# The transposed mask of neighbours: from 64 f16 transposes per graph to ScalarE's sign of a matrix that is already transposed

## The chip, the core and the metric

The kernel runs on one core of one Trainium2 chip. The metric is the device time of one execution in microseconds; the kernel before took 3909.36 us as the median of three runs (3884.14 to 3925.28). TensorE is called PE below, VectorE DVE, ScalarE ACT, GpSimd POOL and SyncE SP.

## The reference

For each of 16 graphs of N = 1024 nodes with 64 features there is a matrix `adj` (1024 x 1024, f32) that is zero where two nodes are not neighbours and otherwise between 0.05 and 1; its diagonal is always positive. Four layers follow one another, each on `h = relu(layernorm(x))`. The first, second and fourth are products with `adj`. The third needs the set of neighbours itself:

```python
nb = (adj_ > 0) & (~eye)[None]
m = nb.sum(-1)
rank = jnp.cumsum(nb, axis=-1) - 1
skip = jnp.where(m > T_THRESH, (m + K_DIL - 1) // K_DIL, 1)
do_dil = (skip > 1) & mask
removed = nb & do_dil[..., None] & ((rank + 1) % skip[..., None] == 0)
rem = removed | jnp.swapaxes(removed, 1, 2)
return jnp.where(rem, 0.0, adj_)
```

Of what is left, each node takes three quantiles over the features of its neighbours, weighted and summed, and a small dense network follows. The change touches the running count (`rank`) alone.

## The kernel before, in words

`direct_path` treats the graphs in six streams of work (`adjacency`, `layers`, `tail`, `gathers`, `neighbour_lists`, `sorts`). They are generators. A loop at the end of the function keeps a model of the engines' clocks (`clk`), takes the first stream that is due by DVE's modelled time and lets it issue its instructions up to its next `yield`. So the order on every engine is fixed when the kernel is built, and several graphs are in work at once: while one graph's mask is made, DVE sorts the gathered neighbours of an earlier one.

`adjacency(b)` works by blocks of 128 rows, i = 0 to 7:

- DVE makes the mask `nb` of the block in f16 (L942) and clears its diagonal (L944). PE transposes the block of `adj` in f32 (L949), ACT copies it out of PSUM into `adjt` (L950), so that `adjt[p, j, i*128 + m]` is `adj[i*128 + m, j*128 + p]`. ACT also sums the mask by halves of a row (L956), into `mn`. DVE adds these sums (L964) and works out `sf`, the numbers that tell which neighbour is dropped (L965 to L971).
- Then the running count, block by block. `flipped(i)` makes the transposed mask `nbt` of block i: eight f16 transposes of `nb` on PE into one PSUM bank (L979) and one ACT copy to SBUF (L980). `flipped(i + 1)` is issued ahead of the work on block i; `nbt` has two buffers. Eight matmuls of `nbt` by a constant staircase (`stair`, L991) give the running count in each half of the row. ACT takes the absolute distance from the count that is dropped (L995) into `gone`, DVE turns it into -1 or 0 (L1000, L1005).
- Then the keys: PE adds the mask, `gone`, its transpose and the node numbers (L1015 to L1023), ACT makes keys of the sum (L1024) and counts them (L1027), and the nodes are sorted by number of neighbours (L1034 to L1073).

`layers(b)` runs beside the last two steps. It normalises (`preln`, L848 to L858), multiplies by `adjt` twice (`messages`, L877, copied by L878), and ACT sums the rows of `adjt` in place (L1212: same shape and same memory in and out, with a sum per row). The next graph's `adjacency` starts once these, and this graph's keys, have been issued. PSUM has three rings: `t` (tiles `pt`, one bank, three buffers), `t2` (two banks, two buffers) and `tm`.

At the end a flag is made from `bad`, which tells of a node with too many or too few neighbours for the lists. If it is set, `general_path` computes everything again in another way.

Of the kernel before, what the change touches and what calls it, by code (L numbers as in the profile page):

```python
# [7 lines left out]
F32 = mybir.dt.float32  # L8
F16 = mybir.dt.float16
BF = mybir.dt.bfloat16  # L10
I32 = mybir.dt.int32
U16 = mybir.dt.uint16
U8 = mybir.dt.uint8
AF = mybir.ActivationFunctionType
ALU = mybir.AluOpType
AX = mybir.AxisListType

P = 128
C = 64
NB = 8  # L20
# [28 lines left out]
BIG = 1e30  # L49

E_ID, E_ONE, E_CAP, E_LOW, E_CN, E_HALF, E_Q, E_END = 0, 128, 256, 264, 272, 280, 288, 352
J_ID, J_BIG, J_OFF, J_ST, J_ROW, J_ONE, J_PI, J_NI, J_END = 0, 128, 256, 384, 896, 1920, 2048, 2176, 2184

# [7 lines left out]
def _wanted(cap, low):  # L63

    places = set()
    for m in range(low, cap + 1):
        above = (cap + 1) // 2 - (m + 1) // 2
        places |= {above + k * (m - 1) // 4 for k in (1, 2, 3)} | {above - k * (1 - m) // 4 for k in (1, 2, 3)}
    return sorted(places)
# [662 lines left out]
def direct_path(ctx: ExitStack, tc: tile.TileContext, t: dict, out: bass.AP, flag):  # L732
# [3 lines left out]
    nc = tc.nc  # L736
    x_in, adj, nodemask = t["x"], t["adj"], t["nodemask"]
    B = x_in.shape[0]

    const = ctx.enter_context(tc.tile_pool(name="const", bufs=1))  # L740
    loads = ctx.enter_context(tc.tile_pool(name="loads", bufs=2))
    graph = ctx.enter_context(tc.tile_pool(name="graph", bufs=1))
    nodes = ctx.enter_context(tc.tile_pool(name="nodes", bufs=2))
# [6 lines left out]
    tt, ts, act = nc.vector.tensor_tensor, nc.vector.tensor_scalar, nc.scalar.activation  # L750
# [4 lines left out]
    ch = const.tile([P, J_END], F16, name="eh")  # L755
    nc.scalar.dma_start(ch, t["eh"])
    identf, onesf = cf[:, E_ID:E_ID + P], cf[:, E_ONE:E_ONE + P]
    cap8, low8, cn8, half8 = (cf[:, e:e + NB] for e in (E_CAP, E_LOW, E_CN, E_HALF))
    identh, big_i, offdiag = (ch[:, e:e + P] for e in (J_ID, J_BIG, J_OFF))
    stair, pidx = ch[:, J_ST:J_ST + N // 2], ch[:, J_PI:J_PI + P]  # L760
    nid = ch[:, J_NI:J_NI + NB]
    jrow, onerow = ch[0:1, J_ROW:J_ROW + N], ch[0:1, J_ONE:J_ONE + P]
    eps = const.tile([P, 1], F32, name="eps")
    nc.vector.memset(eps, 1e-5)
    bad = const.tile([P, NB], F32, name="bad")
    nc.vector.memset(bad, 0.0)

    def weight(name, n):
        w = const.tile([n, t[name].shape[1]], F32, name=name)
        nc.gpsimd.dma_start(w, t[name])  # L770
        return w
# [46 lines left out]
    def after(dve=0.0, pe=0.0, act=0.0, lat=0.3):  # L818

        clk.dve += dve  # L820
        at = clk.dve
        if pe:
            clk.pe = at = max(clk.pe, at) + pe
        if act:
            clk.act = at = max(clk.act, at) + act
        return at + lat


    def bank(dt=F32):
        return psum.tile([P, 2048 // mybir.dt.size(dt)], dt, tag="t", name="pt", bufs=3)  # L830

    def bank2():
        return psum.tile([P, N], F32, tag="t2", name="pt2", bufs=2)
# [101 lines left out]
    def adjacency(b):  # L935
        g = state[b]
        adjt = graph.tile([P, NB, N], F32, name="adjt")
        nb = graph.tile([P, NB, N], F16, name="nb")
        mn = nodes.tile([P, 3, NB], F32, name="mn")
        for i in range(NB):  # L940
# [4 lines left out]
            for q in range(2):  # L945
                p = bank()
                for u in range(4):
                    j = 4 * q + u
# [22 lines left out]
        nc.vector.scalar_tensor_tensor(sf[:, 3], mn[:, 0], 2.0, sf[:, 2], op0=ALU.mult, op1=ALU.add)  # L971
        clk.dve += 0.9
        gone = graph.tile([P, NB, N], F16, name="gone")

        def flipped(i):
            nbt = lists.tile([P, NB, P], F16, name="nbt")
            p = bank(F16)
            for j in range(NB):
                nc.tensor.transpose(p[:, j * P:(j + 1) * P], nb[:, i, j * P:(j + 1) * P], identh)  # L979
            nc.scalar.copy(nbt, p.rearrange("p (j m) -> p j m", m=P))  # L980
            return nbt

        nbt = flipped(0)
        waiting = None
        for i in range(NB):
            following = flipped(i + 1) if i + 1 < NB else None

            p = bank2()
            for j in range(NB):
                o, e = j * P, (j // 4 + 1) * 512  # L990
                nc.tensor.matmul(p[:, o:e], nbt[:, j, :], stair[:, :e - o], start=j % 4 == 0, stop=j % 4 == 3)  # L991

            for q in range(2):
                s = slice(q * 512, (q + 1) * 512)
                act(gone[:, i, s], p[:, s], AF.Abs, bias=sf[:, 2 + q, i:i + 1], scale=2.0)  # L995
            nbt = following
            ready = after(0, pe=3.7, act=2.4, lat=3.0)
            if waiting:
                yield waiting[1]
                ts(gone[:, waiting[0], :], gone[:, waiting[0], :], sf[:, 1, waiting[0]:waiting[0] + 1], -1.0,  # L1000
                   op0=ALU.is_equal, op1=ALU.mult)
                clk.dve += 0.5
            waiting = (i, ready)
        yield waiting[1]
        ts(gone[:, waiting[0], :], gone[:, waiting[0], :], sf[:, 1, waiting[0]:waiting[0] + 1], -1.0,  # L1005
           op0=ALU.is_equal, op1=ALU.mult)
        clk.dve += 0.5
        keys_d = dram.tile([N, N], F16, name="keys_d")
        ms = nodes.tile([P, NB], F32, name="ms")
        for i in range(NB):  # L1010

            p = bank2()
            for q in range(2):
# [4 lines left out]
                for j in range(4 * q, 4 * q + 4):  # L1018
                    d = slice(j * P, (j + 1) * P)
                    nc.tensor.matmul(p[:, d], gone[:, j, i * P:(i + 1) * P], big_i, start=False,  # L1020
                                     stop=j == 4 * q + 3 and i // 4 != q)
# [5 lines left out]
            act(p, p, AF.Sign, accum_out=ms[:, i:i + 1])  # L1027
            yield after(0, pe=4.5, act=2.3) - 4.0

        mv = nodes.tile([P, NB], F32, name="mv")  # L1030
        act(mv, ms, AF.Copy, bias=512.0, scale=0.5)
        yield clk.act + 2.0
        key = nodes.tile([P, NB], F32, name="key")
        nc.vector.scalar_tensor_tensor(key, ms, 512.0, cn8, op0=ALU.mult, op1=ALU.add)  # L1034
        neg = nodes.tile([P, NB], F32, name="neg")
        ts(neg, key, -1.0, None, op0=ALU.mult)
        p = bank2()
        for q in range(2):
# [2 lines left out]
               key[:, 4 * q:4 * q + 4, None].to_broadcast([P, 4, P]), ALU.mult)  # L1041
            nc.tensor.matmul(p[:, q * 512:(q + 1) * 512], onesf, spread.rearrange("p j m -> p (j m)"),
                             start=True, stop=True)
        over = nodes.tile([P, NB], F32, name="over")
        for i in range(NB):
            sink = lists.tile([P, N], F16, tag="ab", name="sink")
            act(sink, p, AF.Sign, bias=neg[:, i:i + 1], accum_out=over[:, i:i + 1])  # L1047
# [1 line left out]
        pos = nodes.tile([P, NB], I32, name="pos", bufs=5)  # L1049
        ts(pos, over, 0.5, 511.5, op0=ALU.mult, op1=ALU.add)  # L1050

        pi = nodes.tile([P, 2, NB], I32, name="pi")
        ts(pi[:, 0], pos, P - 1, None, op0=ALU.bitwise_and)
        ts(pi[:, 1], pos, 7, None, op0=ALU.arith_shift_right)
        ph = nodes.tile([P, 2, NB], F16, name="ph")
        nc.vector.tensor_copy(ph, pi)
        low = lists.tile([P, NB, P], F16, tag="ab", name="low")
        tt(low, pidx[:, None, :].to_broadcast([P, NB, P]), ph[:, 0, :, None].to_broadcast([P, NB, P]), ALU.is_equal)
        high = nodes.tile([P, NB, NB], F16, name="high")
        tt(high, pidx[:, None, :NB].to_broadcast([P, NB, NB]), ph[:, 1, :, None].to_broadcast([P, NB, NB]),  # L1060
           ALU.is_equal)
        both = nodes.tile([P, 2, NB, NB], F16, name="both")
        tt(both[:, 0], high, nid[:, :, None].to_broadcast([P, NB, NB]), ALU.mult)
        tt(both[:, 1], high, mv[:, :, None].to_broadcast([P, NB, NB]), ALU.mult)
        p = bank()
        for i in range(NB):
            nc.tensor.matmul(p[:, :2 * NB].rearrange("p (s k) -> p s k", k=NB), low[:, i, :], both[:, :, i, :],
                             start=i == 0, stop=i == NB - 1)
        m = nodes.tile([P, NB], F32, name="m", bufs=3)
# [332 lines left out]
        done.add(("tail", b))  # L1402


    wcol = const.tile([P, 3], F32, name="wcol")
    for k, w in enumerate((0.25, 0.5, 0.25)):
        nc.vector.memset(wcol[:, k:k + 1], w)
    none = const.tile([P, 2], F32, name="none")
    nc.vector.memset(none[:, :1], BIG)
    nc.vector.memset(none[:, 1:], 0.0)  # L1410
    sizes = [max(p0 + ns * nn for l, p0, _, ns, nn in PACKS if l == k) for k in range(NPACK)]
# [9 lines left out]
    def over_graphs(step, *needs):  # L1421
# [5 lines left out]

    streams = [
        over_graphs(adjacency, ("adjt", 1), ("keys", 1), ("sorts", 3)),
        over_graphs(layers, ("rows", 0), ("tail", 3)),  # L1430
        over_graphs(tail, ("sorts", 0)),
# [23 lines left out]
                assert soonest is not None  # L1455
                clk.dve = soonest

    one = nodes.tile([P, 1], F32, name="one")
    nc.vector.tensor_reduce(one, bad, AX.X, ALU.max)
    p = bank()  # L1460
    nc.tensor.matmul(p[:1, :1], one, onesf[:, :1], start=True, stop=True)
    nc.vector.tensor_copy(flag, p[:1, :1])


@with_exitstack
# [10 lines left out]
def _constants():  # L1476

    import numpy as np

    p = np.arange(P)  # L1480
    ef = np.zeros((P, E_END), np.float32)
    ef[p, E_ID + p] = 1
    ef[:, E_ONE:E_ONE + P] = 1
    e = E_Q
    for b0, n, cap, low, *_ in GROUPS:
        ef[:, E_CAP + b0:E_CAP + b0 + n] = PLACES[b0:b0 + n]
        ef[:, E_LOW + b0:E_LOW + b0 + n] = low
        ef[:, E_HALF + b0:E_HALF + b0 + n] = (cap + 1) // 2
        for q in _wanted(cap, low):
            ef[:, e] = q  # L1490
            e += 1
    for _, _, s0, ns, nn in PACKS:
        ef[:nn, E_CAP] = s0 + ns
    ef[:, E_CN:E_CN + NB] = 512 * N + N - 1 - (p[:, None] + P * np.arange(NB))
    eh = np.zeros((P, J_END), np.float32)
    eh[p, J_ID + p] = 1
    eh[p, J_BIG + p] = 2048
    eh[:, J_OFF:J_OFF + P] = 1
    eh[p, J_OFF + p] = 0
    eh[:, J_ST:J_ST + N // 2] = p[:, None] < np.arange(N // 2)  # L1500
    eh[p, J_ST + p] = 2050
    eh[0, J_ROW:J_ROW + N] = np.arange(N) - 2047
    eh[0, J_ONE:J_ONE + P] = 1
    eh[:, J_PI:J_PI + P] = p
    eh[:, J_NI:J_NI + NB] = p[:, None] + P * np.arange(NB)
    return {**_general_constants(), "ef": ef, "eh": eh.astype(np.float16)}
# [73 lines left out]
```

## Time and profile before

| | |
|---|---|
| median of three runs | 3909.36 us |
| profiled execution | 3897.33 us, span 3895.5 us |
| mean granted PE clock | 0.689 |
| busy: DVE, POOL, PE, ACT | 3035.7, 2644.1, 2044.1, 1410.1 us |
| L979, transposes of the mask | 1024 on PE, 99.8 us busy; first at 32.2 us, last at 3341.2 us |
| L980, copies of the transposed mask | 128 on ACT, 128.2 us busy |

The profile is of one execution. A group's line gives the engine, the operation, what it writes and reads by the program's names, the shape, the count, the busy time, the mean of one in ns, and after a second bar the idle time of the engine just before these instructions and what ended it. An engine's idle time costs something only where work that sets the end waits for it. The profile releases a wait by semaphore events; "remote" and "another core or an unknown queue" mean that it found no releaser, "issue" that the engine waited for nothing that it shows. Some matmul records are missing.

### The profile page before, as it was taken

The page shows a single profiled execution, that of the slowest core. Times are in us where ns is not written, and L with a number is a line of the kernel's source. Part 1 is how long each engine was busy: PE and PEld are TensorE (multiplying, and loading weights), DVE is VectorE, ACT ScalarE, POOL GpSimd, SP SyncE. Part 2 cuts the span into 40 slices and gives each one's busy share as a digit, 9 for nine tenths or more (in the row PEclk, how much of TensorE's full clock was granted, in tenths as well). Part 3 has the DMA queues.
Part 4 walks back from the last instruction along what each step waited for, and adds up shares of the span by engine and source line. Part 5 has one row for each costly group of instructions (what it writes and reads, how often), then busy time and mean ns, then how long its engine had stood idle before and what let it go on. Part 6 is the DMA issues. An engine that isn't in the chain of part 4 may idle for free.

```text
span 3895.5 us, 32579 instructions
## 1 busy us (share of the span) xinstructions
PE 2044.1 (52%) x8483; PEld 988.9 (25%) x8483; DVE 3035.7 (78%) x7309; ACT 1410.1 (36%) x2658; POOL 2644.1 (68%) x2792
## 2 busy tenths in 40 slices
PE   6464554646654574646446474565556555741113
PEld 3222222223222232222222232232222323220101
DVE  1557878879687897888787798899699876979482
ACT  5444334243433434333332443443344433430000
POOL 1077576776667686776776777777778686777781
PEclk8666667677676686676666777767677676765555
DMA  2313234152423425242341524243343423232121
GB/s 89 124 39 115 50 99 117 45 172 46 141 68 101 120 65 154 70 125 69 106 106 45 175 51 153 56 142 80 100 119 104 116 55 123 68 105 58 42 52 55
DMA packets 237348, 362.43 MB, mean 93 GB/s; under 512 B 126848, under 2 KB 128496, under 8 KB 237152
## 3 DMA queue, kind: packets, MB, share of 16 engines
q1 hardware_dynamic: 156912, 255.00, 19.0%
q0 software_dynamic: 80096, 104.70, 13.5%
q8 instruction: 69, 1.13, 0.1%
q14 instruction: 127, 1.04, 0.1%
q10 hardware_dynamic: 144, 0.56, 0.0%
HBM read 245.26 MB, written 114.81 MB: 92 GB/s over the span
## 4 chain that ended last, share of the span: by engine, by line
DVE 42%; issue 14%; PE 12%; another core or an unknown queue 9%; ACT 8%; POOL 8%; DMA 5%; SPq 0%; DVEq 0%; ACTq 0%; POOLq 0%
DVE other L1308 12%; DVE raw L1308 11%; POOL raw L1275 6%; PE pt L877 5%; DVE most L1117 4%; ACT adjt L1212 2%; DVE found L1103 2%; DVE agg L1327 2%; ACT sink L1047 2%; DMA k<-keys_d,node 1%; DMA raw<-h_d,index 1%; PE pt L901 1%; DVE k L1112 1%; DVE nb L942 1%
## 5 line engine op out<-in xcount | busy, mean ns | idle before, releaser
L1275 POOL DMA_INDIRECT raw<-h_d,index x1984 | 2148.8, 1083 | 559.0 <-issue 533.1
L1308 DVE TENSOR_TENSOR other<-raw 128x512 f32<-128x512 f32 (+11 forms) x816 | 536.7, 688 | 151.7 <-DMA raw<-h_d,index 113.9
L877 PE MATMUL pt<-adjt,ha 128*65 128x512 f32 (+1 forms) x1024 | 485.4, 635 | 44.6 <-DVE ha L1199 30.6
L919 POOL COPY gate<-mark 1x1 f32<-1x1 f32 x477 | 163.9, 344 | 416.2 <-DVE mark L917 369.3
L949 PE MATMUL pt<-ef,a 128*128 128x128 f32 x1024 | 207.5, 360 | 320.8 <-ACT adjt L950 129.6
L1308 DVE TENSOR_TENSOR raw<-other 128x512 f32<-128x512 f32 (+10 forms) x464 | 355.9, 792 | 5.8 <-DVE other L1308 0.6
L991 PE MATMUL pt<-eh,nbt 128*128 128x512 f16 (+3 forms) x1024 | 213.8, 365 | 266.5 <-ACT nbt L980 192.2
L1117 DVE MAX8 most<-k 128x8 uint16<-128x1024 uint16 x208 | 255.4, 1228 | 13.2 <-DVE k L1112 3.3
L949 PEld LDWEIGHTS pt<-ef,a 128*128 128x128 f32 x1024 | 157.7, 185 | 408.2 <-issue 180.6
L1024 ACT ACTIVATE nb<-pt 128x1024 f16<-128x1024 f32 x128 | 130.6, 1020 | 317.1 <-remote 118.4
L877 PEld LDWEIGHTS pt<-adjt,ha 128*65 128x65 f32 (+1 forms) x1024 | 148.1, 148 | 364.1 <-issue 360.1
L950 ACT COPY adjt<-pt 128x512 f32<-128x512 f32 x256 | 139.1, 583 | 250.0 <-remote 146.4
L956 ACT ACTIVATE nb<-nb 128x512 f16<-128x512 f16 x256 | 159.6, 629 | 179.3 <-DVE nb L942 70.2
L1308 DVE TENSOR_TENSOR raw<-other,raw 128x640 f32<-128x640 f32 (+3 forms) x448 | 216.5, 494 | 4.9
L1308 DVE TENSOR_TENSOR raw<-raw,other 128x128 f32<-128x128 f32 (+7 forms) x496 | 211.5, 436 | 6.1
L1020 PE MATMUL pt<-eh,gone 128*128 128x128 f16 x1024 | 129.7, 257 | 162.7 <-DVE gone L1000 76.5
L878 ACT COPY big<-pt 64x1024 f32<-64x1024 f32 (+1 forms) x32 | 32.2, 1007 | 496.1 <-PE pt L877 300.6
L1308 DVE TENSOR_TENSOR other<-other,raw 128x128 f32<-128x128 f32 (+4 forms) x448 | 201.4, 460 | 4.2
L1384 PE MATMUL tm<-at,ha 128*64 128x512 f32 x512 | 174.1, 785 | 50.0 <-DMA at<-adjt_d 44.4
L1103 DVE MAX8 found<-k 128x8 f32<-128x1024 f16 x128 | 156.3, 1221 | 51.2 <-DMA k<-keys_d,node 51.2
L991 PEld LDWEIGHTS <-nbt 128*128 128x128 f16 x1024 | 105.0, 116 | 359.4 <-ACT nbt L980 203.2
L1347 POOL DMA_INDIRECT res<-agg_d,pos x128 | 135.7, 1060 | 74.9 <-DMA agg_d<-agg 37.4
(182 smaller groups left out, 4350.6 us busy)
## 6 DMA issues: line engine op xcount, KB each, us to landing
a<-in_adj_dram SPq DMA_DIRECT2D x64, 1024.0 KB
adjt_d<-adjt SPq DMA_DIRECT2D x64, 1024.0 KB
at<-adjt_d SPq DMA_DIRECT2D x128, 512.0 KB
keys_d<-nb SPq DMA_DIRECT2D x64, 512.0 KB
raw<-h_d,index POOLq DMA_INDIRECT x1984
x<-in_x_dram SPq DMA_DIRECT2D x16, 256.0 KB
h_d<-h SPq DMA_DIRECT2D x16, 256.0 KB
agg_d<-agg SPq DMA_DIRECT2D x16, 256.0 KB
```

Of the source, the lines that this page charges most:

```text
L877: nc.tensor.matmul(p[p0:p0 + n, s], h[:, j, :n], adjt[:, j, s], start=j == 0, stop=j == NB - 1)
L919: nc.gpsimd.tensor_copy(opened[:, k % 2:k % 2 + 1], slots[:, k % 8:k % 8 + 1])
L949: nc.tensor.transpose(p[:, u * P:(u + 1) * P], a[:, j * P:(j + 1) * P], identf)
L950: nc.scalar.copy(adjt[:, 4 * q:4 * q + 4, i * P:(i + 1) * P], p.rearrange("p (u m) -> p u m", m=P))
L956: act(nb[:, i, s], nb[:, i, s], AF.Copy, accum_out=mn[:, q, i:i + 1])
L991: nc.tensor.matmul(p[:, o:e], nbt[:, j, :], stair[:, :e - o], start=j % 4 == 0, stop=j % 4 == 3)
L1103: nc.vector.max(out=found[:, o:o + 8], in_=src)
L1117: nc.vector.max(out=most, in_=less.bitcast(U16))
L1275: nc.gpsimd.indirect_dma_start(raw[:, s, i * C:(i + 1) * C], None, h_ds[b % 3], bass.IndirectOffsetOnAxis(ap=g["index"][:, at:at + 1], axi ...
L1308: tt(view(two[to], *((i, vi) if greater else (j, vj)), w), view(two[s], i, vi, w), view(two[u], j, vj, w), ALU.max if greater else ALU.min)
L1347: nc.gpsimd.indirect_dma_start(res[:, i, :], None, g["agg_d"], bass.IndirectOffsetOnAxis(ap=g["pos"][:, i:i + 1], axis=0))
L1384: nc.tensor.matmul(p[q * C:(q + 1) * C, :], ha[:, j, :], even(ats[j], q), start=j == 0, stop=j == NB - 1)
```

## The change

`flipped(i)` takes ACT's sign of block i of `adjt`. As `adjt` keeps the diagonal and the mask `nb` doesn't, block i's own diagonal would be counted: one more matmul per block, of minus the identity by the staircase, takes it out again. The sign of a negative entry would be -1, where the mask has 0; so ACT sums the signs as it goes, DVE compares the sum of all with the number of neighbours plus the diagonal, and any difference sets the flag for the general path. To make room for the new constant and sums, several small tiles get one buffer instead of two, and three small constants share a tile.

```diff
-    identh, big_i, offdiag = (ch[:, e:e + P] for e in (J_ID, J_BIG, J_OFF))
+    identh, big_i, offdiag, minus_i = (ch[:, e:e + P] for e in (J_ID, J_BIG, J_OFF, J_NEG))
...
-    eps = const.tile([P, 1], F32, name="eps")
+    cols = const.tile([P, 8], F32, name="cols")
+    eps, none, wcol = cols[:, :1], cols[:, 1:3], cols[:, 3:6]
...
+    over_all = const.tile([P, NB], F32, name="over_all")
+    nc.vector.memset(over_all, 0.0)
...
+        signs = nodes.tile([P, NB], F32, name="signs", bufs=1)
...
         def flipped(i):
             nbt = lists.tile([P, NB, P], F16, name="nbt")
-            p = bank(F16)
-            for j in range(NB):
-                nc.tensor.transpose(p[:, j * P:(j + 1) * P], nb[:, i, j * P:(j + 1) * P], identh)
-            nc.scalar.copy(nbt, p.rearrange("p (j m) -> p j m", m=P))
+            act(nbt, adjt[:, :, i * P:(i + 1) * P], AF.Sign, accum_out=signs[:, i:i + 1])
             return nbt
...
-                nc.tensor.matmul(p[:, o:e], nbt[:, j, :], stair[:, :e - o], start=j % 4 == 0, stop=j % 4 == 3)
+                nc.tensor.matmul(p[:, o:e], nbt[:, j, :], stair[:, :e - o], start=j % 4 == 0,
+                                 stop=j % 4 == 3 and j != i)
+                if j == i:
+                    nc.tensor.matmul(p[:, o:e], minus_i, stair[:, :e - o], start=False, stop=j % 4 == 3)
...
+        tt(signs, signs, mn[:, 2], ALU.subtract)
+        tt(over_all, over_all, signs, ALU.add)
...
-        mv = nodes.tile([P, NB], F32, name="mv")
+        mv = nodes.tile([P, NB], F32, name="mv", bufs=1)
...
-    one = nodes.tile([P, 1], F32, name="one")
-    nc.vector.tensor_reduce(one, bad, AX.X, ALU.max)
+    one = nodes.tile([P, 2], F32, name="one", bufs=1)
+    nc.vector.tensor_reduce(one[:, :1], over_all, AX.X, ALU.add)
+    ts(one[:, :1], one[:, :1], -1.0, float(B * NB), op0=ALU.mult, op1=ALU.add)
+    nc.vector.tensor_reduce(one[:, 1:], bad, AX.X, ALU.max)
+    tt(one[:, :1], one[:, :1], one[:, 1:], ALU.add)
     p = bank()
-    nc.tensor.matmul(p[:1, :1], one, onesf[:, :1], start=True, stop=True)
-    nc.vector.tensor_copy(flag, p[:1, :1])
+    nc.tensor.matmul(p[:1, :1], one[:, :1], onesf[:, :1], start=True, stop=True)
+    ts(flag, p[:1, :1], 1.0, None, op0=ALU.min)
```

The tiles `key`, `neg`, `over`, `pi`, `ph`, `high` and `both` get one buffer as `mv` does.

More of the change, by code (lines that the diff above doesn't have):

```diff
@@ L51 @@
 E_ID, E_ONE, E_CAP, E_LOW, E_CN, E_HALF, E_Q, E_END = 0, 128, 256, 264, 272, 280, 288, 352
-J_ID, J_BIG, J_OFF, J_ST, J_ROW, J_ONE, J_PI, J_NI, J_END = 0, 128, 256, 384, 896, 1920, 2048, 2176, 2184
+J_ID, J_BIG, J_OFF, J_ST, J_ROW, J_ONE, J_PI, J_NI, J_NEG, J_END = 0, 128, 256, 384, 896, 1920, 2048, 2176, 2184, 2312
 PLACES = [21, 19, 17, 16, 15, 13, 12, 11]
@@ L1028, in adjacency @@
             yield after(0, pe=4.5, act=2.3) - 4.0
-        mv = nodes.tile([P, NB], F32, name="mv")
+        mv = nodes.tile([P, NB], F32, name="mv", bufs=1)
         act(mv, ms, AF.Copy, bias=512.0, scale=0.5)
         yield clk.act + 2.0
-        key = nodes.tile([P, NB], F32, name="key")
+        key = nodes.tile([P, NB], F32, name="key", bufs=1)
         nc.vector.scalar_tensor_tensor(key, ms, 512.0, cn8, op0=ALU.mult, op1=ALU.add)
-        neg = nodes.tile([P, NB], F32, name="neg")
+        neg = nodes.tile([P, NB], F32, name="neg", bufs=1)
         ts(neg, key, -1.0, None, op0=ALU.mult)
@@ L1043, in adjacency @@
                              start=True, stop=True)
-        over = nodes.tile([P, NB], F32, name="over")
+        over = nodes.tile([P, NB], F32, name="over", bufs=1)
         for i in range(NB):
@@ L1050, in adjacency @@
         ts(pos, over, 0.5, 511.5, op0=ALU.mult, op1=ALU.add)
-        pi = nodes.tile([P, 2, NB], I32, name="pi")
+        pi = nodes.tile([P, 2, NB], I32, name="pi", bufs=1)
         ts(pi[:, 0], pos, P - 1, None, op0=ALU.bitwise_and)
         ts(pi[:, 1], pos, 7, None, op0=ALU.arith_shift_right)
-        ph = nodes.tile([P, 2, NB], F16, name="ph")
+        ph = nodes.tile([P, 2, NB], F16, name="ph", bufs=1)
         nc.vector.tensor_copy(ph, pi)
@@ L1058, in adjacency @@
         tt(low, pidx[:, None, :].to_broadcast([P, NB, P]), ph[:, 0, :, None].to_broadcast([P, NB, P]), ALU.is_equal)
-        high = nodes.tile([P, NB, NB], F16, name="high")
+        high = nodes.tile([P, NB, NB], F16, name="high", bufs=1)
         tt(high, pidx[:, None, :NB].to_broadcast([P, NB, NB]), ph[:, 1, :, None].to_broadcast([P, NB, NB]),
            ALU.is_equal)
-        both = nodes.tile([P, 2, NB, NB], F16, name="both")
+        both = nodes.tile([P, 2, NB, NB], F16, name="both", bufs=1)
         tt(both[:, 0], high, nid[:, :, None].to_broadcast([P, NB, NB]), ALU.mult)
@@ L1402, in tail @@
         done.add(("tail", b))
-    wcol = const.tile([P, 3], F32, name="wcol")
     for k, w in enumerate((0.25, 0.5, 0.25)):
         nc.vector.memset(wcol[:, k:k + 1], w)
-    none = const.tile([P, 2], F32, name="none")
     nc.vector.memset(none[:, :1], BIG)
@@ L1497, in _constants @@
     eh[p, J_BIG + p] = 2048
+    eh[p, J_NEG + p] = -1
     eh[:, J_OFF:J_OFF + P] = 1
```

## The prediction

> **What bounds the kernel now.** I read the page first, for busy shares and the chain, then the list of waits of VectorE (DVE), then the groups by form around the change, then a table of windows that cut each graph's stage of the change out of the span, and last the timeline of the first such stage.
>
> ```profile
> PE 2044.1 (52%) x8483; PEld 988.9 (25%) x8483; DVE 3035.7 (78%) x7309; ACT 1410.1 (36%) x2658; POOL 2644.1 (68%) x2792
> ...
> DVE 42%; issue 14%; PE 12%; another core or an unknown queue 9%; ACT 8%; POOL 8%; DMA 5%; SPq 0%; DVEq 0%; ACTq 0%; POOLq 0%
> ```
>
> DVE leads in busy time and on the chain. One execution of 16 graphs takes 3895.5 us, so a graph passes about every 220 us (the stages below start that far apart), 190 of them DVE work. Every engine works off a fixed order, so what counts is where DVE waits:
>
> ```profile
> DVE other L1308 <- DMA raw<-h_d,index: 113.9, 17, 25.7
> DVE stat L853 <- ACT mid L851: 96.3, 14, 16.8
> DVE stat L856 <- ACT stat L854: 64.3, 9, 19.0
> DVE gone L1000 <- ACT gone L995: 52.5, 10, 15.7
> ```
>
> (us in total, times, longest.) Only the last of these belongs to the stage of the change. With 6.4 us "issue" before L1000 and 1.7 us before L1005 it is 60.6 us, the most that a faster stage could give DVE directly. In the timeline these waits lie in four graphs: 30.6 us in the first, about 24 in the second, 4.2 in the eleventh, 1.6 in the fourteenth; in twelve of sixteen graphs DVE never waits for `gone`. The two long ones (15.69 and 13.44 us) are not the transposes' either: ScalarE (ACT) is held just ahead by `big` L878, which waits for the messages' matmuls L877. Windows cut around the stage of the third to the sixteenth graph (786 us together) have DVE busy 719 us, 91%. Two of them:
>
> ```profile
> 2445.00:2501.00 56.00, 25.77 (x164) 15.03 (x164) 50.71 (x136) 27.61 (x50) 39.01 (x40) 0.67 0.27 56
> 2655.00:2704.00 49.00, 22.19 (x147) 12.63 (x146) 47.89 (x132) 20.32 (x34) 39.41 (x39) 0.71 0.25 42
> ```
>
> (window, length, busy us and instructions of PE, PEld, DVE, ACT, POOL, granted clock, DMA share, GB/s.) PE and ACT have about half of the stage free. After it the wait goes the other way: PE's L1020 waits for DVE's L1000 and L1005, 115.4 us in 24 times. So a `gone` that ACT finishes earlier is not used earlier. The rows that the change deals in:
>
> ```profile
> L991 PE MATMUL pt<-eh,nbt 128*128 128x512 f16 x256 | 122.8, 480 | 258.8 <-ACT nbt L980 192.2 <-issue 35.5 <-ACT mid L851 16.7
> L979 PE MATMUL pt<-eh,nb 128*128 128x128 f16 x1024 | 99.8, 254 | 54.0 <-ACT adjt L950 30.8 <-issue 18.7 <-ACT x L1378 4.5
> L980 ACT COPY nbt<-pt 128x1024 f16<-128x1024 f16 x128 | 128.2, 1013 | 79.5 <-remote 54.8 <-PE pt L979 14.8 <-PE pt L991 4.7
> L1212 ACT ACTIVATE adjt<-adjt 128x1024 f32<-128x1024 f32 x128 | 133.2, 1044 | 0.0
> L1212 ACT ACTIVATION_READ_ACCUMULATOR adjt<-adjt 128x1 f32 x128 | 24.2, 189 | 0.0
> ```
>
> **What the skill says.** "ScalarE: Activation LUTs", What ACT_TABLE_LOAD costs: an activation passes one element per cycle whatever the function, 186 ns + 0.833 ns per element with immediate operands, so about 1039 ns for 1024. The trace agrees: 1044 ns (L1212), 1019 ns for the Sign of L1027. Same page, Table sets: cheap functions such as relu, copy and abs sit in every set. Sign is not named there, but the trace has loads only at the square root (17, L854), the tanh (16, L1192) and the start, though Sign runs at L1027 and L1047 in every graph; the built order of the changed kernel has no load more. "TensorE: Matmul & The Clock Gate", HAM clock gate: the clock halves after some 3.4 us of idleness and recovers after as much work. The trace agrees in kind: eight transposes span 0.61 us at 48.94 and 1.06 us at 44.02, eight L991 matmuls 1.25 us at 47.85 and 2.31 us at 41.92.
>
> **The change, part by part.** Apart from what follows, the built orders of all five engines are the same instruction by instruction; POOL's and SP's are identical.
>
> 1. PE loses 1024 f16 transposes (L979) and their weight loads: 99.8 and 81.6 us busy, per step of eight 0.6 us warm to 1.0 cold. It gains 128 matmuls of minus identity by staircase, one per step, of 512, 384, 256 or 128 columns. The four widths of L991 cost 122.8 + 103.1 + 83.4 + 64.5 = 373.8 us for 1024, so 128 cost 46.7, 0.15 us (1.25/8) to 0.3 us (2.31/8) per step. Net -53 us of PE. PE is not the bound; I count 0. Bounds: 0 to the whole 31.5 us that the first rival works out.
>
> 2. ACT: 128 copies out of PSUM become 128 Signs of `adjt` with a sum. No row shows a Sign of strided f32 from SBUF. From below: no dearer than the copy. From above: L1212's rows added, 1044 + 189 = 1233 ns, 0.22 more than 1013. In sequence they overlap: two copies take 1.91 us at 40.87, so the second starts 0.90 after the first; eight L1212 with their sums take 8.32 us in the chain, 1.04 each. I take +0.14 us each, 1.1 per graph, 18 in all (bounds 0 and 28). The stride I cost at nothing: L950 writes the same strided pattern in 583 ns, L887 and L1391 a plain one in 580 and 584. The 18 us lie beside DVE work in 12 of 16 graphs; where DVE waits for `gone`, they are 1 us per graph. Queued behind a Sign on ACT are the two Abs (L995) and sometimes L851 or L854 of the layers, for which DVE waits in this stage only in the first two graphs (4.1, 2.9 and 2.3 us).
>
> 3. The waits: ACT stood idle before L980 for 79.5 us, nearly all of it for PE; Sign waits for ACT's own earlier writes only. The buffer of two rows ago is free because the Abs ahead in the queue has waited for the matmuls that read it. But the two Abs right behind need the staircase of the same PE, so the wait moves one instruction on. What is left: where PE is late, the first staircase starts without two transposes and a copy ahead of it (about 1.5 to 2 us earlier), given back at 0.14 per step. Where ACT is late (PE waits 192.2 us for `nbt`, 48 times) it is 0.14 later. I count -1 us over the first two graphs for this and +1 for step 2.
>
> 4. DVE gains two operations on 128x8 per graph (`signs` and `over_all`). The 128x8 ops at 40.22 to 41.50 take 0.16 to 0.17 us and start up to 0.21 apart when each needs the last: 0.4 per graph, 6.4 in all. They stand behind the last L1005, whose wait covers the last Sign, so they add no wait. DVE is the bound: all 6.4 counted. At the end three small operations more: 0.6.
>
> 5. PSUM ring `pt`: eight allocations fewer per graph. No wait for `pt` on an L980 release shows, so 0. Single buffers for `mv`, `key`, `neg`, `over`, `pi`, `ph`, `high`, `both`: the old reader is a graph (220 us) back, 0. The constants' DMA grows by 128 of 2184 columns and lands before its first use: 0. Scheduler clock: the entries that order the streams are untouched.
>
> Sum: 0 - 1 + 1 + 6.4 + 0.6 = +7 us, against this execution's 3897.33 us (span 3895.5 and 1.8 around it) 3904; the median of the runs, 3909.36, lies 12 above that execution, and I carry the difference over: 3916, no change that can be told.
>
> **Rivals.** (a) Faster: the stage's chain does hold DVE. All waits for `gone` but those behind the messages go: 60.6 - 15.7 - 13.4 = 31.5, giving 3909 + 7 - 31.5 = 3885. For: ACT stood 79.5 us before L980. Against: twelve graphs without a wait. To pass 1% a share of the 160 us of L853 and L856 waits would have to shrink too; a quarter gives 3845. (b) Slower: PE goes cold. With fewer instructions between waits for `nbt` the staircases run at the half clock: 2.31 + 0.3 = 2.6 us per step, where ACT's step, a Sign and two Abs (1.04 + 1.27), is 2.3. From there PE decides; against the 2.2 of before (0.90 + 1.27) a step is 0.45 longer, 3.6 us per graph, 58 if none of it is covered: 3909 + 7 + 58 = 3974. For: the clock is only 0.62 to 0.79 in these windows. Against: cold steps exist now and cost 2.31 + 1.0, more than 2.6. (c) ACT's upper bound, all on the path: 3909 + 7 + 28 = 3944, still within 1%. (d) The sum of signs doesn't match and the general path runs as well: far slower, no row prices it. Against: the sum is over whole numbers and the diagonal is positive in these inputs.
>
> **How the numbers follow.** Forecast 0.52, (a) 0.18, (b) 0.16, (c) 0.12, (d) 0.02. A measurement tells about 1% from no change (the three runs before span 3884 to 3925). Of the forecast 0.48 falls within 1% and 0.02 on each side; of (a) 0.11 is faster by more; of (c) 0.03 slower by more; (b) and (d) are slower. So 0.13, 0.64, 0.23. The range 3862 to 3970 holds the forecast, (c), the nearer part of (a) and the milder half of (b), and leaves out about 2 in 10.
>
> **What would show it.** Right: Sign near 1.04 us plus 0.19 and no more table loads; PE busy some 50 us less; PE's waits for `nbt` about as long; the wait before Sign gone and longer before L995; DVE busy about 6 us more, its waits for `gone` still in the first graphs. Wrong: a Sign of 1.5 us or more, a granted clock lower by 0.03 and staircases mostly near 2.3 us, or DVE's waits for L851, L854 and `gone` changed by over 40 us together.

## The result and the profile after

Over 20 runs each the changed kernel takes 3891.72 us and the kernel before 3898.16 us (medians): ratio 0.9987, with a 95% interval of 0.9965 to 1.0009, that is -14 to +3.5 us, no difference that can be told. (The median of the three runs known before the prediction, 3909.36, lay high among the twenty.) On two further, steadier chips one series each gives 1.0007 (0.9999 to 1.0015) and 1.0009 (1.0003 to 1.0016) of about 3660 us, or +3 us; the second of them is clear of its own noise, by 1 to 6 us. That the change is near nothing holds. The numbers put on it, +7 us and a time of 3916 us, do not: +7 lies outside all three intervals.

The page of the changed kernel, busy time and chain:

```profile
PE 2010.3 (52%) x7587; PEld 934.0 (24%) x7587; DVE 3040.5 (78%) x7345; ACT 1424.2 (37%) x2786; POOL 2650.6 (68%) x2792
...
DVE 42%; issue 16%; POOL 10%; PE 10%; another core or an unknown queue 9%; ACT 9%; DMA 4%; SPq 0%; DVEq 0%; ACTq 0%; POOLq 0%
```

PE is busy 33.8 us less (2044.1 before), the weight loads 54.9 less, ACT 14.1 more, DVE 4.8 more, and DVE keeps its 42% of the chain. DVE's waits, the rows that answer to those of before:

```profile
DVE stat L858 <- ACT mid L856: 105.6, 11, 36.3
DVE other L1316 <- DMA raw<-h_d,index: 103.6, 13, 25.8
...
DVE gone L1006 <- ACT gone L1001: 35.9, 8, 17.0
...
DVE stat L861 <- ACT stat L859: 30.4, 6, 14.1
```

L1006 is the old L1000, L858 the old L853, L861 the old L856. The wait for `gone` fell from 52.5 to 35.9 us and that for L861 from 64.3 to 30.4, while L858 rose by 9.3: one profile of each, and such rows move by tens of us between profiles of one kernel (L858: 105.6 us here, 67.2 in a later profile of the changed kernel on another chip). The groups of the change, by form:

```profile
L983 ACT ACTIVATE nbt<-adjt 128x1024 f16<-128x1024 f32 x128 | 134.9, 1055 | 0.1
L994 PE MATMUL pt<-eh,nbt 128*128 128x512 f16 x256 | 129.0, 504 | 322.1 <-ACT nbt L983 256.1 <-issue 63.4 <-PE pt L994 2.5
L1001 ACT ACTIVATE gone<-pt,sf 128x512 f16<-128x512 f32 x256 | 161.6, 685 | 104.7 <-remote 35.1 <-PE pt L994 27.0 <-DVE other L1316 11.6
...
L983 ACT ACTIVATION_READ_ACCUMULATOR nbt<-adjt 128x1 f32 x128 | 25.4, 198 | 0.0
L997 PE MATMUL pt<-eh 128*128 128x512 f16 x32 | 17.5, 546 | 0.0
```

The 79.5 us that ACT stood idle before the copy have become 0.1 us before the Sign, and the wait has moved on. Before the two Abs ACT stood idle for 55.8 us (L995), now for 104.7 (L1001). For 54.8 of the 79.5 and 35.1 of the 104.7 the profile has no releaser. The Abs before:

```profile
L995 ACT ACTIVATE gone<-pt,sf 128x512 f16<-128x512 f32 x256 | 162.5, 690 | 55.8 <-PE pt L991 31.0 <-issue 8.8 <-PE pt L979 6.6
```

PE, which no longer has transposes to do, waits longer for ACT: 256.1 us for `nbt` against 192.2.

### The profile page after: what moved, and what is told of

It reads as the page before. It is cut to its first block, busy times and chain, and to the rows that moved or that the text cites. A ratio compares the mean times of both kernels' runs of the same rounds, so it can differ in the third digit from the quotient of the medians.

```text
span 3890.7 us, 30892 instructions
## 1 busy us (share of the span) xinstructions
PE 2010.3 (52%) x7587; PEld 934.0 (24%) x7587; DVE 3040.5 (78%) x7345; ACT 1424.2 (37%) x2786; POOL 2650.6 (68%) x2792
## 4 chain that ended last, share of the span: by engine, by line
DVE 42%; issue 16%; POOL 10%; PE 10%; another core or an unknown queue 9%; ACT 9%; DMA 4%; SPq 0%; DVEq 0%; ACTq 0%; POOLq 0%
DVE other L1316 11%; DVE raw L1316 10%; POOL raw L1283 8%; DVE most L1125 5%; PE pt L882 4%; DVE found L1111 2%; DVE agg L1335 2%; ACT adjt L1220 2%; ACT sink L1055 2%; DVE k L1120 1%; DMA k<-keys_d,node 1%; POOL res L1355 1%; PE pt L906 1%; DVE nb L947 1%
## 5 line engine op out<-in xcount | busy, mean ns | idle before, releaser
L994 PE MATMUL pt<-eh,nbt 128*128 128x512 f16 (+3 forms) x1024 | 238.3, 381 | 322.1 <-ACT nbt L983 256.1
L1001 ACT ACTIVATE gone<-pt,sf 128x512 f16<-128x512 f32 x256 | 161.6, 685 | 104.7 <-remote 35.1
```

## Experiments

Twelve runs were made, of nine edits and, twice more, of the changed kernel, each beside the kernel before on the same chip. The first four shared a chip on which that kernel takes 3834.08 us. The other eight ran four each on two chips on which it takes 3660.64 and 3659.19 us, with narrower intervals; these two are called the steady chips, the second one the chip of `before_dve8`, `sign3`, `nosum2` and `after_third`. The changed kernel did not run on the chip of the first four, so its 0.9987 is borrowed there from the first comparison, and differences from it are rougher than the intervals shown. In the expectations "Theory A" and "B" are said anew for each run.

**The prices of the three engines, on the first of these chips.** Sixteen more pairs of small DVE operations; the transposes doubled; the Sign doubled.

```diff
         tt(over_all, over_all, signs, ALU.add)
+        spare = nodes.tile([P, 2, NB], F32, name="spare", bufs=1)
+        for k in range(16):
+            tt(spare[:, 0], signs, mn[:, 2], ALU.subtract)
+            tt(spare[:, 1], spare[:, 0], mn[:, 2], ALU.add)
```

> The changed kernel with 16 more pairs of 128x8 operations on DVE behind the two new ones, into a tile that nobody reads: 512 operations, at 0.2 us each 102 us of DVE in all, at the very place where the change adds 32. Theory A (DVE is the bound, its operations there count one for one, as the prediction had it): ratio to the kernel before 0.9987 + 0.026 = 1.025. Theory B (DVE has other waits, 744 us, that swallow part of what is put in its queue): half or less of it, 1.012 or below.

1.0171 (1.0133 to 1.0209). Against the changed kernel's 0.9987 that is 0.0184, 71 us for 512 operations: 0.14 us each (about 0.11 to 0.17 by both intervals), between the two theories.

```diff
             for j in range(NB):
                 nc.tensor.transpose(p[:, j * P:(j + 1) * P], nb[:, i, j * P:(j + 1) * P], identh)
+            for j in range(NB):
+                nc.tensor.transpose(p[:, j * P:(j + 1) * P], nb[:, i, j * P:(j + 1) * P], identh)
```

> The kernel before with every block's eight f16 transposes made twice into the same bank: 1024 transposes more, 100 us of PE by the group's busy time. Theory A (PE's part is worth nothing): ratio 1.000, within 0.002. Theory B (the transposes hold up ACT and through it DVE): taking them away was worth some 12 us and adding as many costs as much or more, 1.003 to 1.008.

1.0027 (1.0009 to 1.0045), 10 us (3 to 17): on this chip 100 us of PE weren't free, as Theory B has it. In the profile the idle time before the copy is 208.8 us (79.5 in the kernel before, whose profile comes from the first comparison), but 146.0 of it has no releaser and only 44.3 are put down to the transposes, so how the 10 us came about isn't shown:

```profile
L982 ACT COPY nbt<-pt 128x1024 f16<-128x1024 f16 x128 | 128.8, 1012 | 208.8 <-remote 146.0 <-PE pt L981 44.3 <-PE pt L993 11.2
```

```diff
-            act(nbt, adjt[:, :, i * P:(i + 1) * P], AF.Sign, accum_out=signs[:, i:i + 1])
+            act(nbt, adjt[:, :, i * P:(i + 1) * P], AF.Sign)
+            act(nbt, adjt[:, :, i * P:(i + 1) * P], AF.Sign, accum_out=signs[:, i:i + 1])
```

> The changed kernel with each Sign of the transposed block issued twice (the first without its sum, into the same tile): 128 more, 133 us of ACT, 1.04 per step. Theory A (ACT is covered by DVE's work except in the first two graphs, where 17 us of it show): 1.003. Theory B (ACT's extra time reaches DVE through the layers' operations queued behind it in every graph): half or more of it, 1.016 to 1.033.

1.0018 (0.9995 to 1.0041), 0.0031 above the changed kernel: 12 us for 133 of ACT, nine tenths of them covered, near Theory A. By both intervals it is 0 to 24 us; Theory B is out.

**The check for negative entries.**

```diff
-            act(nbt, adjt[:, :, i * P:(i + 1) * P], AF.Sign, accum_out=signs[:, i:i + 1])
+            act(nbt, adjt[:, :, i * P:(i + 1) * P], AF.Sign)
...
-        tt(signs, signs, mn[:, 2], ALU.subtract)
-        tt(over_all, over_all, signs, ALU.add)
...
```

> The changed kernel without the check for negative entries: no sum on the Sign, no two DVE operations per graph, the flag from the list bounds alone. Theory A (DVE counts one for one): 6.4 us of DVE and 0.1 us of ACT per Sign less, 0.9987 - 0.0018 = 0.997. Theory B (neither reaches the end): 0.9987.

0.9997 (0.9974 to 1.0019): too wide to part the two. It ran again later, on a steady chip and with the changed kernel beside it:

> The changed kernel without its check for negative entries, once more, beside the changed kernel on the same chip: the two DVE operations per graph and the sum on each Sign taken away. Theory A: 6.4 us and more below the changed kernel, 0.002 of the time. Theory B: 4.4 us, 0.001. Theory C: no difference, within 0.0008.

> The changed kernel on the same chip as the three others, as their foot. Theory A: 7 us over the kernel before, 1.002. Theory B (the sum with the smaller prices): 2 to 3 us, 1.0007. Theory C (transposes worth something, the additions nothing): 5 us below, 0.9987.

0.9995 (0.9986 to 1.0003) without the check, 1.0009 (1.0003 to 1.0016) with it. Without its check the change costs nothing that can be told (-5 to +1 us): the Signs, the matmuls of minus identity, the missing transposes and the single buffers come to about zero together. The matmuls of minus identity and the single buffers were not tried alone. The difference between the two points is 0.0014 or 5 us, and their intervals only just touch: by both it is 1 to 9 us, which doesn't part 6.4 from 4.4. The +3.3 us of the whole change (1.1 to 5.9) lie below `after_third`'s Theory A with its 7 and fit its Theory B.

**DVE's part alone**, eight times over, in the kernel before:

```diff
+        spare = nodes.tile([P, 2, NB], F32, name="spare", bufs=1)
+        for k in range(8):
+            tt(spare[:, 0], mn[:, 0], mn[:, 2], ALU.subtract)
+            tt(spare[:, 1], spare[:, 0], mn[:, 2], ALU.add)
         keys_d = dram.tile([N, N], F16, name="keys_d")
```

> The kernel before with only DVE's part of the change, eight times over: eight pairs of 128x8 operations per graph at the place where the change has one, 256 operations. Theory A (each counts with its 0.2 us from start to start, as the prediction had it): 51 us, ratio 1.013 to 1.014. Theory B (the price that 512 of them showed, 0.14 us): 35 us, 1.009. Theory C (a DVE that waits elsewhere swallows a small addition): under 15 us, 1.004 or less.

1.0072 (1.0059 to 1.0086): 26.4 us (21.6 to 31.5) for 256 operations, 0.10 us each (0.084 to 0.12), less than Theory B's 35 and more than Theory C's 15. Their groups in the profile:

```profile
L1010 DVE TENSOR_TENSOR spare<-mn 128x8 f32<-128x8 f32 x128 | 22.2, 174 | 3.8
L1011 DVE TENSOR_TENSOR spare<-spare,mn 128x8 f32<-128x8 f32 x128 | 21.4, 167 | 4.4
```

They are busy 43.6 us and 8.2 us idle stands before them, 51.8 in all, the 0.2 us from start to start that the prediction used. Half of it reaches the end. By which path isn't shown. PE's group behind them, the first step of the keys, has a wait that is put down to the added operations; but the changed kernel on the same chip, with one pair per graph in place of eight, has one just as long in its place, and PE reads neither tile:

```profile
L1024 PE MATMUL pt<-eh,gone 128*128 128x128 f16 x1024 | 128.4, 252 | 198.1 <-DVE gone L1000 109.8 <-DVE gone L1005 39.3 <-DVE spare L1010 25.3
```

```profile
L1028 PE MATMUL pt<-eh,gone 128*128 128x128 f16 x1024 | 124.6, 248 | 192.5 <-DVE gone L1006 107.0 <-DVE gone L1011 38.1 <-DVE signs L1014 25.3
```

DVE's idle stretches in the timeline sum to 497 us in this profile and to 518 to 525 in two of the changed kernel and one of the kernel with four times the transposes on the steady chips (one profile each). So part of what was added was taken out of idle time. That these are waits that end with another engine or a DMA and so don't move is the likely reason, not shown.

**ACT and PE pushed further, on the steady chips.** The Sign issued three times:

> The changed kernel with every Sign issued three times, 256 more, 266 us of ACT, 2.1 us per step on top of 2.3. Theory A (ACT's price goes on in proportion: 12 us for the first 133): about 24 us over the changed kernel beside it, ratio near 1.006. Theory B (beyond twice the step DVE waits for the mask in every graph): 1.02 or more.

1.0049 (1.0036 to 1.0063), 0.0040 above the changed kernel beside it: 15 us (9 to 20) for 266 us of ACT, under Theory A's 24. Theory B is out. The transposes four times, in the kernel before:

> The kernel before with every block's eight transposes made four times: 3072 more, 300 us of PE. A step of PE is then about 3.7 us warm against 2.2 of ACT. Theory A (the doubling's 10 us for 100 us of PE go on in proportion): 1.008. Theory B (beyond the point where PE's step is longer than ACT's, DVE waits in every graph): 1.5 us times 8 times 16 = 190 us less what DVE's own work covers, 1.02 or more.

1.0008 (1.0000 to 1.0017), 3 us (0 to 6) for three times as many transposes added as in the doubling; their three groups are busy 260 us. Theory B is out and Theory A too high: on this chip PE's time is all but free.

The transposes put back into the changed kernel, for nobody:

```diff
+            p = bank(F16)
+            for j in range(NB):
+                nc.tensor.transpose(p[:, j * P:(j + 1) * P], nb[:, i, j * P:(j + 1) * P], identh)
             act(nbt, adjt[:, :, i * P:(i + 1) * P], AF.Sign, accum_out=signs[:, i:i + 1])
```

> The changed kernel with the eight f16 transposes of every block put back into a PSUM bank that nobody reads: the PE part of the change undone, ACT still takes its Sign from the transposed adjacency and waits for no transpose. Theory A (what the transposes cost was PE's time ahead of the staircase matmuls): as dear as the doubling in the kernel before, 10 us, ratio 0.9987 + 0.0027 = 1.0014. Theory B (what they cost was ACT's copy standing behind them): nothing, 0.9987.

> The changed kernel itself, on the same chip and beside the same runs as the three others. All theories: 0.9987, 0.9965 to 1.0009.

1.0010 (1.0002 to 1.0018) against 1.0007 (0.9999 to 1.0015) for the changed kernel itself. The intervals overlap: on this chip putting the transposes back costs nothing that can be measured. It doesn't part the two theories, since PE's price here is already near nothing.

**A faster version.** As the mask of these inputs is symmetric, block i's transposed mask is the mask's own column block. Neither transposes nor copies nor Signs are needed:

```diff
-        nbt = flipped(0)
...
-                nc.tensor.matmul(p[:, o:e], nbt[:, j, :], stair[:, :e - o], start=j % 4 == 0, stop=j % 4 == 3)
+                nc.tensor.matmul(p[:, o:e], nb[:, j, i * P:(i + 1) * P], stair[:, :e - o], start=j % 4 == 0, stop=j % 4 == 3)
```

> The kernel before without any transposition of the mask: the staircase matmuls take the mask's column block itself as weights, which is the same matrix only because the mask of these inputs is symmetric. No transposes (100 us of PE), no copies (128 us of ACT), no wait between them, nothing added on DVE. Theory A (small prices as measured: 10 us for 100 of PE, some 12 for 133 of ACT): 22 us, ratio 0.994. Theory B (DVE's own work covers the stage, so that there is nothing to be had): 0.998 to 1.000.

0.9975 (0.9966 to 0.9984): 9 us less, faster than both kernels, though less than Theory A's 22 and just at the edge of Theory B. Its page:

```profile
PE 1973.4 (54%) x7459; PEld 918.1 (25%) x7459; DVE 3035.1 (83%) x7309; ACT 1287.9 (35%) x2530; POOL 2643.7 (72%) x2792
```

ACT is busy 132.6 us less than in the changed kernel beside it (1420.5); with PE's share and the DVE operations that it doesn't have this is worth 12 us against it. It holds only for a symmetric mask, which the kernel would have to check.

## Why the prediction was right or wrong

**What held.** DVE bounds the kernel and the stage lies in its cover. In parts 2 and 3 of the sum the Sign takes 1055 and 198 ns and from start to start 1.04 us (first stage, 40.94 and 41.98), as estimated. ACT's 14.1 us more, at sign3's price (15 us for 266), are 0.8 us; +1 was counted. The changed kernel loads tables 17 and 16 times in these two groups, as before. The wait did move one instruction on, to the Abs:

```profile
L859 ACT ACT_TABLE_LOAD x17 | 21.8, 1283 | 0.3
L1200 ACT ACT_TABLE_LOAD x16 | 20.5, 1283 | 0.3
```

**The step that failed is part 4.** "DVE is the bound: all 6.4 counted" takes 32 operations at 0.2 us one for one. before_dve8 measured 0.10 us for each, so 3.3 us if one pair per graph costs an eighth of eight pairs (one pair alone was not tried). The 0.2 us was right as the time that an operation holds DVE; what was wrong was to let all of it reach the end, though DVE is busy for only 78% to 83% of the span. The busy share was read as if it were 100%.

**The foot was wrong too.** Of the 24 us between 3916 and the measured 3891.72, 11 are the distance of the three runs' median from that of the twenty (3909.36 and 3898.16). The sum itself was made against the profiled execution of 3897.33, close to the twenty; carrying the 12 us over made it worse. The other 13 us are +7 against -6.4, of which part 4 explains about 2 to 3; the rest is within that comparison's noise.

**Part 1, a zero, was right on the steady chips only.** There PE's time is worth 0.01 us per us (before_t4: 3 for 260). On the chip of the first four runs it was worth 0.10 (before_t2). With the busy time that the change was to save, 53 us, these are -0.6 and -5 us. (PE's busy time fell by only 33.8 us: the four widths of the staircase take 390.3 us where they took 373.8.) The sum with measured prices, DVE 3.3, ACT 0.8, end 0.6 as estimated, PE -0.6, is an estimate of +4 us on the steady chips, where +3.3 was measured; part 3's -1 is left out, as the price of the transposes should contain it. On the chip of the first four, DVE at dve16's 0.14 gives 4.5, ACT at sign2's 12 for 133 gives 1.3, the end 0.6 and PE -5: about +1 us. If these prices hold for the first comparison too, where the kernel before takes 3898 us and not 3834, that is inside its -14 to +3.5, in which 7 is not. That the -6 us between the medians there are more than scatter isn't shown.

**Rivals.** (a) had DVE's waits for `gone` go. They fell from 52.5 to 35.9 us, but nothing shows this to be the change's doing: on a steady chip the kernel before with its added DVE operations has 35.8 us of them and the changed kernel 37.8, each in nine waits in the first two graphs, the longest (17 us) behind the messages. First the old design (before_dve8), then the changed kernel (after_third):

```profile
DVE gone L1000 <- ACT gone L995: 35.8, 9, 17.2
```

```profile
DVE gone L1006 <- ACT gone L1001: 37.8, 9, 17.1
```

The same holds for a sign of being wrong that did appear in the first pair of profiles: the three waits (96.3, 64.3 and 52.5 us before, 105.6, 30.4 and 35.9 after) changed by 41 us together. On the steady chips their sum is 113 and 119 us in two profiles of the old design with added work (before_dve8, before_t4), 116 and 119 in two of the changed kernel. Nor were the 79.5 us before the copy "nearly all" PE's, as part 3 has it: 54.8 of them had no releaser, and on the steady chip of before_dve8 19.9 us stand there:

```profile
L980 ACT COPY nbt<-pt 128x1024 f16<-128x1024 f16 x128 | 128.0, 1013 | 19.9 <-PE pt L979 19.8
```

(b) came true in its direction, far less in its size, and not in its price: the granted clock fell from 0.689 to 0.679, a third of the 0.03 that was to show it, and a staircase matmul of 512 columns took 504 ns instead of 480 (515 in after_third, 481 in before_dve8), with no loss that shows. Even three Signs per block, where these matmuls take 569 ns, cost 15 us and not 58. (c), ACT's whole time on the path, is off by sign3. (d) did not happen.

The table of windows, with PE and ACT about half free, pointed the right way for both on the steady chips.

## What to carry to other kernels

An operation put into the queue of the engine that leads in busy time need not be paid in full: here DVE was busy for 83% of the span, and half of each added operation reached the end (0.10 of 0.2 us). Putting it in many times over is a quick way to learn that part. Work taken from an engine that the bound engine waits for in few places can be worth next to nothing, however busy the list of groups makes it look: three Signs per block in place of one cost 15 us for 266. A before and an after profile taken once each can differ by more than the change does; profiles of both designs on another chip told the two apart. And before a wait is counted as removed, ask for what the instruction behind it waits.

## What the runs showed of the hardware

The same kernel before took 3898.16, 3834.08, 3660.64 and 3659.19 us on different chips or at different times, 6% from end to end, far more than any edit here. DVE's work is the same (busy 3040.5 and 3038.8 us in two profiles of the changed kernel); its idle stretches sum to 744 us in the first and 520 in the second. What sets the two profiles apart is waits, most of them ACT's, to which the trace gives no releaser. The group of ACT's copies of the adjacency, in the first profile and in the last:

```profile
L955 ACT COPY adjt<-pt 128x512 f32<-128x512 f32 x256 | 140.3, 585 | 282.6 <-remote 148.0 <-issue 47.3 <-PE pt L954 38.2
```

```profile
L955 ACT COPY adjt<-pt 128x512 f32<-128x512 f32 x256 | 136.6, 581 | 52.7 <-DMA adjt_d<-adjt 32.0 <-PE pt L954 20.5
```

At 1747.7 us of the first profile, for instance, ACT stands still for 16.05 us in front of such a copy, though the last transposes recorded before it had ended at 1747.1. On the steady chips "remote" is gone, from this row and from all waits listed for the eight profiles there, and the chain that ended last looks otherwise. In the profile of after_third (42% DVE, 9% ACT, 10% PE and 9% without a releaser in the first profile of the same kernel):

```profile
DVE 60%; POOL 12%; issue 11%; PE 7%; DMA 7%; ACT 3%; SPq 0%; DVEq 0%; POOLq 0%; ACTq 0%
```

What these pauses are stays open; no run here tells. They may be why PE's time had a price on one chip and almost none on the others, but that is argued, not shown.

The Sign, which waits for nothing, also shows that reading a strided f32 block (runs of 128 out of 1024) costs ACT little here: 1055 ns against 1044 for the unbroken rows of L1212 before.
